# Cross attention with its projections in other places, self-attention with scores 512 columns wide

## The chip, the core and the metric

The kernel runs on one core of a Trainium2 chip. The metric is the device time of one execution in microseconds (us). A core has five engines that the profile names: PE (TensorE, matrix products; its weight loads are listed as PEld), DVE (VectorE), ACT (ScalarE), POOL (GpSimd) and SP, which here only issues DMAs. Each engine works through its own queue in order; an instruction waits at the head of its queue until the semaphores that it names have reached their values, and everything behind it waits with it. PE writes its products to PSUM, which the program hands out in banks of 512 fp32 values for each of 128 partitions; the other engines read them from there.

## The reference, cut to what matters

The program is a decoder of four layers. x is [16, 256, 128] (16 batches of 256 tokens, 128 features), the context ctx is [16, 64, 128]. Each layer has a mixing block, a cross attention against ctx and a feed-forward block, each followed by a residual sum and a layer norm over the 128 features. All that the change touches is softmax attention with 16 heads of 8 features:

```python
q = proj(Q, Wq, bq); k = proj(K, Wk, bk); v = proj(V, Wv, bv)     # heads: [B, 16, S, 8]
scores = einsum('bhqd,bhkd->bhqk', q, k) * (1 / sqrt(8))
attn = softmax(scores, axis=-1)
out = einsum('bhqk,bhkd->bhqd', attn, v)
return merge_heads(out) @ Wo.T + bo
```

Layers 0, 2 and 3 (x0, x2, x3 below) have a cross attention of this kind, with x as Q and ctx as K and V; layer 0's has no bias ahead of Wo, layer 3's adds a mask to the scores. Layer 3 is an encoder block as well: its cross attention is followed by a self-attention in which Q, K and V all come from x (256 keys instead of 64). Layer 1 has other code.

## The kernel before

**Layout.** The residual stream lies in SBUF twice: `xt` with tokens on the partitions, and `xT` with features on the partitions (128 rows, 4096 token columns). A group g is 512 tokens, that is two batches, 2g and 2g+1. `transposed(g)` (L348 to L353) makes a group's part of `xT` from `xt`: four PE transposes (L341) into one PSUM bank `m`, then one ACT copy (L353).

**Heads.** A head has 8 features, so four heads lie in each 32 rows of PE. A product runs in four row tiles i = 0 to 3 of 32 rows; within one tile the four heads j are told apart by a masked copy (`hm4`), which holds the features of one head and zeros for the other three. POOL makes that copy. One of the two operands of the scores must be masked.

**Order.** Each block runs under `in_order`: PE executes its instructions exactly as the program writes them. The other engines' instructions are ordered by a scheduler, by when their data comes. PSUM is handed out by name: in `banks(sc=(2, 2), y=(1, 1), ...)` the first number says how many tiles of that name there are, the second how many banks each has. A new tile takes the place of the oldest of its name and waits until its last reader is done.

**`cross_attention`** (L521) loops over batches b with helpers that are issued ahead of their use:

- `queries(g)` (L554): one product of 512 columns into `m`, and the copy to `qT` on DVE (`evac_dve`, L643 to L648), for two batches.
- `values(g)` (L540): four products into `m` for four batches, spread by DVE into one of two `vx` tiles (L552 with a bias, else L549).
- `keys(b)` (L560): the masked copy `kb` on POOL.
- `scores(b)` (L564): 8 fp32 products `sc<-qT,kb` of 256 columns, then two ACT exponentials of 1024 elements (`e`, L576). With a mask (layer 3), DVE adds it for one half and ACT for the other, ahead of the exponentials.
- `sums(b)` (L585): the products of `e` with `vx` and with ones (`nd`), then `normalized` on DVE: reciprocal (L1967) and product `oTn` (L1969).
- `out_product(b)` (L633): two products `y<-oTn`. After an odd batch `finish` follows: residual sum with a bias (POOL L433, DVE L456 or L1761), `norm` (L384: statistics on DVE L391 and L392, reciprocal root on POOL L379 and L381, `nm` on POOL L396 and L397, four scalings on ACT L402). The scalings are put off to `settle()` in the next round.
- `transposed(b//2-2)` for odd b from 5 on. In layer 0 a `side` runs the end of the layer's mixing block between these steps.

In layers 2 and 3 there are two `nd` tiles and one `m`; in layer 0 one `nd` and two `m`. A round is, on PE: `scores(b+1)`, `sums(b)`, `queries(b//2+1)` in even b, `values(b//4+1)` where b % 4 is 1, `out_product(b-1)`, `transposed` in odd b.

**`self_attention`** (L1854) loops over batches n and head index j, with `aside(n, j)` between the scores of the next step and the sums of this one:

```python
with s.banks(sc=(3, 2), nd=(1, 1), m=(1, 1)), s.in_order():
    ...
            for j in range(4):
                if n < B and (n, j) != (B - 1, 3):
                    scores(n + j // 3, (j + 1) % 4)
                aside(n, j)
                if n < B:
                    sums(n, j)
```

- `scores(n, j)` (L1894) computes one head of each of the four row tiles: for each half t of the keys, the masked keys `kb4` of head j are PE's weights and the 256 queries are streamed. Each of the 8 fp32 products shows as two matmul instructions. Two ACT exponentials follow (L1903).
- `sums(n, j)` (L1905): 8 products with `vxs` (values with columns of ones between), into one `nd` tile for each batch. After j=3: a copy `nds` (DVE L1914), the sums picked out and their reciprocal `rcs` (L1915 to L1918), the numerators `vas` on POOL (L1921, L1922).
- `divided(n)` (L1924): a product `m<-rcs,cst` that swaps columns, then `oTs = vas * m` on DVE (L1928).
- `batch(n)` (L1882): the values of a batch into `m` (`m<-w_x,xT`), four DVE sums into `vxs` (L1888), and the masked keys on POOL (L1892).
- `project` (L1876): `qT` or `kTs` for a group, into `m`, with a DVE copy.
- `out(g)` (L1930): four products into `m`, then `finish` (residual sum L1761, `norm` with the scalings on DVE L405, two products on POOL).

Asides by place, all through the single bank `m`: even n has `project` k at j=0, `divided(n-1)` at j=1, `batch(n+1)` at j=2, `project` q at j=3; odd n has `out` at j=0, `divided` at j=1, `batch` at j=2, `transposed` at j=3.

Of the kernel before, what the change touches and what calls it, by code (L numbers as in the profile page):

```python
# [16 lines left out]
ALU = mybir.AluOpType  # L17
# [503 lines left out]
def cross_attention(s, wq, wk, wv, wo, bq, bk, bv, finish, mask=None, side=None):  # L521

    nc = s.nc
    kT = s.lp.tile([128, B * SC], FP, name=s.nm("kT"))

    vxs = [s.lp.tile([128, 4, 4, 96], FP, name=s.nm("vx")) for _ in range(2)]
    for t in vxs:
        nc.gpsimd.memset(t, 0.0)
    on = s.c["on2"].rearrange("p (u k) -> p u k", u=2)
    hm4 = s.c["hm4"].unsqueeze(2).broadcast_to([128, 4, SC])
    q, kb, es, oT, y = {}, {}, {}, {}, {}

    def values(g):
        ps = s.bank("m")
        for j in range(4):  # L540
            s.mm(ps[:, 128 * j:128 * j + 128], s.ctx2[:, 4 * g + j, :, :].rearrange("p a k -> p (a k)"), wv)
        v = ps.rearrange("p (b i u a d) -> p (b i) u a d", b=4, i=4, u=2, a=2)
        dst = vxs[g % 2].rearrange("p b i (u x) -> p (b i) u x", u=2)
        for a in range(2):
            r = slice(64 * a, 64 * a + 64)
            da = dst[r, :, :, 8 * a:8 * a + 8]
            if bv is None:
                nc.vector.tensor_copy(da, v[r, :, :, a, :])
            else:  # L549
                row = bv[r, :].rearrange("p (i u a d) -> p i u a d", i=4, u=2, a=2)[:, :, :, a, :]  # L550
                for j in range(4):
                    nc.vector.tensor_tensor(da[:, 4 * j:4 * j + 4], v[r, 4 * j:4 * j + 4, :, a, :], row, ALU.add)  # L552

    def queries(g):  # L554
        ps = s.bank("m")
        s.mm(ps, wq, s.xT[:, 512 * g:512 * g + 512])
        q[g] = s.work("qT", [128, 512])
        evac_dve(s, q[g], ps, bq)

    def keys(b):  # L560
        kb[b] = s.work("kb", [128, 4, SC])
        nc.gpsimd.tensor_tensor(kb[b], kT[:, SC * b:SC * b + SC].unsqueeze(1).broadcast_to([128, 4, SC]), hm4, ALU.mult)

    def scores(b):  # L564
        qb = q[b // 2][:, 256 * (b % 2):256 * (b % 2) + 256]
        sc = [s.bank("sc", [128, 2, 2, S]) for _ in range(2)]
        for u in range(2):
            for i in range(4):
                r = slice(32 * i, 32 * i + 32)
                s.mm(sc[i // 2][:, i % 2, u, :],  # L570
                     kb[b][r, 2 * u:2 * u + 2, :].rearrange("p j k -> p (j k)"), qb[r, :])
        e = es[b] = s.work("e", [128, 4, 2, S])
        for h in range(2):
            eu = e[:, 2 * h:2 * h + 2, :, :]
            if mask is None:
                s.latest = nc.scalar.activation(eu, sc[h], AF.Exp, scale=8 ** -0.5)  # L576
            else:
                mk, nmx = mask
                if h == 0:
                    nc.vector.tensor_scalar(eu, sc[h], 8 ** -0.5, mk[:, b:b + 1], ALU.mult, ALU.add)  # L580
                else:
                    nc.scalar.activation(eu, sc[h], AF.Identity, scale=8 ** -0.5, bias=mk[:, b:b + 1])
                s.latest = nc.scalar.activation(eu, eu, AF.Exp, bias=nmx[:, b:b + 1])

    def sums(b):  # L585

        nd = s.bank("nd", [128, 2, S])
        vx = vxs[b // 4 % 2]
        for w in range(2):
            for u in range(2):  # L590
                for i in range(4):
                    s.mm(nd[32 * i:32 * i + 32, w, :], on[:, u, :] if w else vx[:, b % 4, i, 32 * u:32 * u + 32],
                         es[b][:, i, u, :], u == 0, u == 1)
        oT[b] = normalized(s, nd)

    if side is None:
        side = lambda b, late: None
        few, more = 2, 1
    else:
        few, more = 1, 2  # L600
    with s.banks(sc=(2, 2), nd=(few, 1), y=(1, 1), m=(more, 1)), s.in_order(), s.deferring():
        side(-1, False)
        for g in range(2):
            ps = s.bank("nd")
            s.mm(ps, wk, s.ctx2[:, 8 * g:8 * g + 8, 0, :])
            evac(s, kT[:, 512 * g:512 * g + 512], ps, bk)
        values(0)
        side(-1, True)
        queries(0)
        keys(0)  # L610
        keys(1)
        scores(0)
        for b in range(B + 6):
            if b + 1 < B:
                scores(b + 1)
            s.settle()
            side(b, False)
            if b < B:
                sums(b)
            side(b, True)  # L620
            if b + 2 < B:
                keys(b + 2)
                if b % 2 == 0:
                    queries(b // 2 + 1)
                if b % 4 == 1 and b + 3 < B:
                    values(b // 4 + 1)
            if 1 <= b <= B:
                out_product(s, y, oT, b - 1, wo, finish)
            if b % 2 == 1 and b >= 5 and b // 2 - 2 < NG:
                s.transposed(b // 2 - 2)  # L630

# [1222 lines left out]
def self_attention(s, wq, wk, wv, wo, bq, bk, bv, finish):  # L1854
# [5 lines left out]

    nc = s.nc

    vxs = [s.lp.tile([128, 2, 4, 128], FP, name=s.nm("vs")) for i in range(3)]
# [5 lines left out]
    hm4 = s.c["hm4"].unsqueeze(2).broadcast_to([128, 4, S])  # L1871
    lo, hi = s.c["half"][:, 0:1], s.c["half"][:, 1:2]
    row = bv.rearrange("p (i j d) -> p i j d", i=4, j=4)
    q, k, kb, es, oT, nd, va, rc = {}, {}, {}, {}, {}, {}, {}, {}

    def project(d, n, g, wt, bias):  # L1876
        ps = s.bank("m")
# [1 line left out]
        d[g] = s.work(n, [128, 512])  # L1879
        evac_dve(s, d[g], ps, bias)  # L1880

    def batch(n):  # L1882
        ps = s.bank("m", [128, 2, 256])
        for t in range(2):
            s.mm(ps[:, t, 0:128], s.xT[:, S * n + 128 * t:S * n + 128 * t + 128], wv)
        pv = ps[:, :, 0:128].rearrange("p t (i j d) -> p t i j d", i=4, j=4)
        for j in range(4):
            nc.vector.tensor_tensor(vxs[n % 3][:, :, :, 40 * j:40 * j + 8], pv[:, :, :, j, :],  # L1888
                                    row[:, :, j, :].unsqueeze(1).broadcast_to([128, 2, 4, 8]), ALU.add)
        kb[n] = s.work("kb4", [128, 4, S])  # L1890
        o = S * (n % 2)
        nc.gpsimd.tensor_tensor(kb[n], k[n // 2][:, o:o + S].unsqueeze(1).broadcast_to([128, 4, S]), hm4, ALU.mult)  # L1892

    def scores(n, j):  # L1894
        o = S * (n % 2)
        sc = [s.bank("sc", [128, 2, 2, S]) for _ in range(2)]
        for t in range(2):
            for i in range(4):
                r = slice(32 * i, 32 * i + 32)
                s.mm(sc[i // 2][:, i % 2, t, :], kb[n][r, j, 128 * t:128 * t + 128], q[n // 2][r, o:o + S])  # L1900
        e = es[n, j] = s.work("e", [128, 4, 2, S])
        for h in range(2):
            nc.scalar.activation(e[:, 2 * h:2 * h + 2, :, :], sc[h], AF.Exp, scale=8 ** -0.5)  # L1903

    def sums(n, j):  # L1905
        if j == 0:
            nd[n] = s.bank("nd", [128, 2, S])
        for t in range(2):
            for i in range(4):
                s.part(nd[n][32 * i:32 * i + 32, j // 2, :], vxs[n % 3][:, t, i, 32 * j:32 * j + 32],  # L1910
                       es[n, j][:, i, t, :], j == t == 0, j % 2 == 1 and t == 1)
        if j == 3:
            sb = s.work("nds", [128, 2, S])
            nc.vector.tensor_copy(sb, nd[n])  # L1914
            d = rc[n] = s.work("rcs", [128, S])  # L1915
            nc.vector.tensor_scalar(d, sb[:, 0, :], hi, None, ALU.mult)
            nc.vector.scalar_tensor_tensor(d, sb[:, 1, :], lo, d, ALU.mult, ALU.add)
            nc.vector.reciprocal(d, d)  # L1918
            va[n] = s.work("vas", [128, S])
            for u, m in enumerate((lo, hi)):  # L1920
                nc.gpsimd.tensor_scalar(sb[:, u, :], sb[:, u, :], m, None, ALU.mult)  # L1921
            nc.gpsimd.tensor_tensor(va[n], sb[:, 0, :], sb[:, 1, :], ALU.add)  # L1922

    def divided(n):  # L1924
        ps = s.bank("m", [128, 2, S])
        s.mm(ps[:, 0, :], s.c["swap"], rc[n])
        oT[n] = s.work("oTs", [128, S], bufs=4)
        nc.vector.tensor_tensor(oT[n], va[n], ps[:, 0, :], ALU.mult)  # L1928

    def out(g):  # L1930
        y = s.bank("m", [128, 4, D])
# [4 lines left out]
    def aside(n, j):  # L1936

        g = n // 2
        if j == 1 and 1 <= n <= B:
            divided(n - 1)  # L1940
        if j == 2 and n + 1 < B:
            batch(n + 1)
        if n % 2 == 0 and j in (0, 3) and g + 1 < NG:
            project(*((q, "qT", g + 1, wq, bq) if j else (k, "kTs", g + 1, wk, bk)))
        if n % 2 == 1 and j == 0 and 1 <= g <= NG:
            out(g - 1)
        if n % 2 == 1 and j == 3 and 2 <= g <= NG + 1:
# [2 lines left out]
    with s.banks(sc=(3, 2), nd=(1, 1), m=(1, 1)), s.in_order():  # L1950
        project(q, "qT", 0, wq, bq)
        project(k, "kTs", 0, wk, bk)
        batch(0)
        scores(0, 0)
        for n in range(B + 4):
            for j in range(4):
# [49 lines left out]
```

## Time and profile before

| | before |
|---|---|
| time, median of 3 runs | 2239.61 us (2233.31 to 2247.02) |
| the profiled execution: its own time | 2240.24 us |
| the profiled execution: span of the profile | 2238.4 us |
| mean granted PE clock over the span | 0.874 of full speed |
| instructions | 39466 |
| DVE busy groups with most time | L1624 75.1 us, L1967 84.1 us, L391 119.7 us |
| ACT's exponentials in self-attention (L1903) | 128 of 1021 ns |

The profile is of one execution. Its views give times in microseconds from the start of the span. A line of a group or of a timeline names the engine, the program line, the operation, its output and inputs (`out<-in`) with their shapes (partitions x elements), a count (`x16`), and in brackets the idle time of the engine just before with what ended it. "L334" is the helper that issues every plain matrix product, so products are told apart by their tiles. Matmul records of one engine overlap: PE has row tiles that run beside each other, so a step's length is best read from the start of one group to the start of the next. A view by windows gives, for each stretch: the window, its length, busy time and number of instructions of PE, weight loads, DVE, ACT and POOL, then the granted clock, the share of the DMA engines and their rate.

### The profile page before, as it was taken

What the parts mean: (1) busy time and instruction counts of PE and PEld (TensorE: products, weight loads), DVE (VectorE), ACT (ScalarE), POOL (GpSimd) and SP (SyncE); (2) the same over time, 40 slices, a digit from 0 to 9 for tenths busy, and PEclk for the clock granted to TensorE, in tenths of its full rate; (3) what the DMA queues carried; (4) which work ended last, traced back from release to release, by engine and by line L of the source; (5) the groups of instructions that cost most, each with busy time, mean ns of one, the idle gap of its engine ahead of it and who ended that gap; (6) DMA issues with size and microseconds to landing.
All of it is one profiled execution on the core that took longest, in us unless ns stands there. A gap on an engine that the chain in (4) does not pass through costs nothing.

```text
span 2238.4 us, 39466 instructions
## 1 busy us (share of the span) xinstructions
PE 1801.0 (80%) x16572; PEld 1135.4 (51%) x16572; DVE 1133.3 (51%) x2808; ACT 857.8 (38%) x1267; POOL 810.5 (36%) x956
## 2 busy tenths in 40 slices
PE   6784378886999826859784799987879998999998
PEld 3451256664777714636452566654445544555554
DVE  5677625554466663145476767746725552322231
ACT  6565633432433201322353222225646654233221
POOL 2432322222344225756334334434535653121110
PEclk8896579997999956979896789988979998999999
DMA  3000000001001212430000000010000000000000
GB/s 113 4 3 21 1 2 3 3 2 45 11 29 29 66 46 47 78 82 1 6 15 20 1 1 1 2 36 29 2 1 2 2 1 1 5 5 5 5 10 10
DMA packets 45649, 41.59 MB, mean 19 GB/s; under 512 B 6880, under 2 KB 42144, under 8 KB 44832
## 3 DMA queue, kind: packets, MB, share of 16 engines
q1 hardware_dynamic: 35456, 31.22, 4.5%
q0 software_dynamic: 5632, 4.33, 1.5%
q10 hardware_dynamic: 4384, 3.52, 0.5%
q8 instruction: 130, 2.13, 0.4%
q14 instruction: 47, 0.39, 0.1%
HBM read 28.44 MB, written 10.62 MB: 17 GB/s over the span
## 4 chain that ended last, share of the span: by engine, by line
PE 55%; DVE 16%; POOL 12%; issue 9%; ACT 5%; DMA 2%; POOLq 0%; SPq 0%; DVEq 0%; ACTq 0%
PE p L334 14%; PE m L334 12%; PE sc L334 11%; PE y L334 6%; PE nd L334 3%; POOL rs L381 2%; PE nd L338 2%; DVE rcT L1967 2%; PE den L338 2%; PE m L341 2%; POOL acc L1316 2%; DVE st L391 1%; PE num L334 1%; ACT xt L402 1%; DVE r L456 1%
## 5 line engine op out<-in xcount | busy, mean ns | idle before, releaser
L334 PE MATMUL p<-h,w_f 128*128 128x512 f32 x512 | 222.3, 592 | 0.4 <-DVE h L1818 0.4
L334 PE MATMUL sc<-qT,kb 32*128 32x256 f32 (+1 forms) x2816 | 182.8, 378 | 42.5 <-DVE qT L648 16.1
L379 POOL TENSOR_SCALAR ve<-mv 128x4 f32<-128x4 f32 x128 | 30.5, 238 | 425.9 <-DVE mv L392 422.4
L334 PEld LDWEIGHTS sc<-qT,kb 32*128 32x128 f32 x2816 | 127.7, 201 | 94.4 <-issue 61.1
L341 PE MATMUL m<-ident,xt 128*128 128x128 f32 x448 | 87.8, 319 | 104.7 <-ACT xt L402 48.4
L334 PEld LDWEIGHTS p<-h,w_f 128*128 128x128 f32 x512 | 96.7, 190 | 119.8 <-issue 117.9
L1903 ACT ACTIVATE e<-sc 128x1024 f32<-128x1024 f32 x128 | 124.0, 1021 | 74.2 <-PE sc L334 73.4
L381 POOL TENSOR_TENSOR rs<-ve,nhalf 128x4 f32<-128x4 f32 x128 | 134.0, 1047 | 6.3
L341 PEld LDWEIGHTS m<-ident,xt 128*128 128x128 f32 x448 | 59.3, 156 | 133.5 <-ACT xt L402 55.6
L391 DVE BATCH_NORM_STATS2 st<-r 128x6 f32<-128x128 f32 x480 | 119.7, 272 | 3.2
L433 POOL TENSOR_TENSOR xb<-xt,r_x 128x512 f32<-128x512 f32 x48 | 60.8, 1272 | 155.9 <-DVE r L1761 78.4
L1967 DVE RECIPROCAL rcT<-nd 128x256 f32<-128x256 f32 x48 | 84.1, 1751 | 64.5 <-PE nd L334 64.5
L353 ACT COPY xT<-m 128x512 f32<-128x512 f32 x104 | 59.9, 581 | 134.0 <-PE m L341 133.4
L402 ACT ACTIVATE xt<-r,nm,rs 128x128 f32<-128x128 f32 x176 | 72.5, 484 | 94.7 <-POOL nm L397 63.7
L1823 ACT ACTIVATE h<-p,w_f 128x512 f32<-128x512 f32 x64 | 44.0, 687 | 163.4 <-PE p L334 163.3
L334 PE MATMUL m<-xT,w_a 128*128 128x512 f32 x144 | 81.7, 682 | 25.8 <-DVE vxs L908 18.8
L405 DVE TENSOR_SCALAR xt<-r,mv,rs 128x128 f32<-128x128 f32 x208 | 65.8, 378 | 59.6 <-POOL rs L381 59.6
L1829 DVE TENSOR_TENSOR ys<-y,r_f 128x512 f32<-128x512 f32 x8 | 5.5, 691 | 175.4 <-PE y L334 175.4
L576 ACT ACTIVATE e<-sc 128x1024 f32<-128x1024 f32 x64 | 61.9, 1019 | 62.8 <-PE sc L334 62.8
L1624 DVE TENSOR_TENSOR a<-sc,cst 128x1024 f32<-128x1024 f32 x64 | 75.1, 1209 | 14.7 <-PE sc L334 14.7
L392 DVE BATCH_NORM_AGGREGATE mv<-st 128x2 f32<-128x6 f32 x512 | 80.9, 167 | 0.1
L1092 ACT ACTIVATE e<-sc 128x1024 f32<-128x1024 f32 x32 | 32.8, 1024 | 110.0 <-PE sc L334 110.0
(423 smaller groups left out, 4086.3 us busy)
## 6 DMA issues: line engine op xcount, KB each, us to landing
acc<-xt SPq DMA_DIRECT2D x16, 256.0 KB, 2.8
mw<-in_moe SPq DMA_DIRECT2D x8, 512.0 KB, 3.7
yx<-acc SPq DMA_DIRECT2D x12, 256.0 KB, 3.4
w_f<-in_w_f SPq DMA_DIRECT2D x1, 2824.0 KB, 10.6
w_x<-in_w_x SPq DMA_DIRECT2D x1, 2336.5 KB, 9.8
xt<-in_x SPq DMA_DIRECT2D x8, 256.0 KB, 7.4
rows<-xn SPq DMA_DIRECT2D x8, 256.0 KB, 2.4
out_x<-xt SPq DMA_DIRECT2D x8, 256.0 KB, 2.3
```

Source lines behind the costliest of these rows:

```text
L334: self.put(self.nc.tensor.matmul(out=out, lhsT=lhsT, rhs=rhs, start=start, stop=stop))
L338: self.put(self.nc.tensor.matmul(out=out, lhsT=lhsT, rhs=rhs, start=start, stop=stop, skip_group_check=True))
L341: self.put(self.nc.tensor.transpose(out, in_, self.ident if ident is None else ident))
L381: nc.gpsimd.tensor_tensor(rs, ve, self.nhalf[:, :n], ALU.pow)
L391: nc.vector.bn_stats(st[:, j, :], r[:, j, :])
L392: nc.vector.bn_aggr(mv[:, j, :], st[:, j, :])
L402: ins, front = nc.scalar.activation(out[:, j, :], r[:, j, :], AF.Identity, bias=nm[:, j:j + 1], scale=rs[:, j:j + 1]), self.latest
L405: ins, front = nc.vector.tensor_scalar(out[:, j, :], r[:, j, :], mv[:, j, 0:1], rs[:, j:j + 1], ALU.subtract, ALU.mult), self.mark
L576: s.latest = nc.scalar.activation(eu, sc[h], AF.Exp, scale=8 ** -0.5)
L1624: s.mark = nc.vector.tensor_tensor(a[:, h, :, :], sc[h].rearrange("p i j k -> p (i j) k"), tri, ALU.mult)
L1903: nc.scalar.activation(e[:, 2 * h:2 * h + 2, :, :], sc[h], AF.Exp, scale=8 ** -0.5)
L1967: s.nc.vector.reciprocal(rc, nd[:, 1, :])
```

## The change

In `cross_attention` two calls move within a round: `queries(b//2+1)` from after the sums to before them, in the same even rounds; `values(b//4+1)` from the rounds with b % 4 = 1 to those with b % 4 = 2, and from before `out_product` to after it.

In `self_attention` the mask goes to the other operand: POOL makes masked queries `qb` (tile name still `kb4`) instead of masked keys. The weights of a scores product are then 128 keys without a mask, and the streamed operand is two heads' masked queries, 512 columns. A step (n, j) now holds the key half t = j % 2 for two heads instead of both halves for one head; there are 4 products of 512 columns for 8 of 256. `sums` follows this order with the same products. `divided(n-1)` and `batch(n+1)` now share one `m` tile, a half of the bank each, one behind the other at j=1. `project` q is at j=0 of even n and k at j=2; j=3 of even n and j=2 of odd n have no aside.

```diff
@@ cross_attention, the loop over b
             s.settle()
             side(b, False)
+            if b % 2 == 0 and b + 2 < B:
+                queries(b // 2 + 1)
             if b < B:
                 sums(b)
             side(b, True)
             if b + 2 < B:
                 keys(b + 2)
-                if b % 2 == 0:
-                    queries(b // 2 + 1)
-                if b % 4 == 1 and b + 3 < B:
-                    values(b // 4 + 1)
             if 1 <= b <= B:
                 out_product(s, y, oT, b - 1, wo, finish)
+            if b % 4 == 2 and b + 2 < B:
+                values(b // 4 + 1)
             if b % 2 == 1 and b >= 5 and b // 2 - 2 < NG:
                 s.transposed(b // 2 - 2)
@@ self_attention
-    def batch(n):
-        ps = s.bank("m", [128, 2, 256])
+    def batch(n, ps):
         for t in range(2):
-            s.mm(ps[:, t, 0:128], s.xT[:, S * n + 128 * t:S * n + 128 * t + 128], wv)
+            s.mm(ps[:, t, :], s.xT[:, S * n + 128 * t:S * n + 128 * t + 128], wv)
...
-        kb[n] = s.work("kb4", [128, 4, S])
+        qb[n] = s.work("kb4", [128, 4, S])
         o = S * (n % 2)
-        nc.gpsimd.tensor_tensor(kb[n], k[n // 2][:, o:o + S].unsqueeze(1).broadcast_to([128, 4, S]), hm4, ALU.mult)
+        nc.gpsimd.tensor_tensor(qb[n], q[n // 2][:, o:o + S].unsqueeze(1).broadcast_to([128, 4, S]), hm4, ALU.mult)
 
     def scores(n, j):
-        o = S * (n % 2)
+        o = S * (n % 2) + 128 * (j % 2)
         sc = [s.bank("sc", [128, 2, 2, S]) for _ in range(2)]
-        for t in range(2):
-            for i in range(4):
-                r = slice(32 * i, 32 * i + 32)
-                s.mm(sc[i // 2][:, i % 2, t, :], kb[n][r, j, 128 * t:128 * t + 128], q[n // 2][r, o:o + S])
+        for i in range(4):
+            r = slice(32 * i, 32 * i + 32)
+            s.mm(sc[i // 2][:, i % 2, :, :].rearrange("p h k -> p (h k)"), k[n // 2][r, o:o + 128],
+                 qb[n][r, j - j % 2:j - j % 2 + 2, :].rearrange("p h k -> p (h k)"))
...
-        for t in range(2):
+        t = j % 2
+        for u in range(2):
             for i in range(4):
-                s.part(nd[n][32 * i:32 * i + 32, j // 2, :], vxs[n % 3][:, t, i, 32 * j:32 * j + 32],
-                       es[n, j][:, i, t, :], j == t == 0, j % 2 == 1 and t == 1)
+                h = j - t + u
+                s.part(nd[n][32 * i:32 * i + 32, j // 2, :], vxs[n % 3][:, t, i, 32 * h:32 * h + 32],
+                       es[n, j][:, i, u, :], j == u == 0, t == u == 1)
...
-    def divided(n):
-        ps = s.bank("m", [128, 2, S])
-        s.mm(ps[:, 0, :], s.c["swap"], rc[n])
+    def divided(n, ps):
+        s.mm(ps, s.c["swap"], rc[n])
         oT[n] = s.work("oTs", [128, S], bufs=4)
-        nc.vector.tensor_tensor(oT[n], va[n], ps[:, 0, :], ALU.mult)
+        nc.vector.tensor_tensor(oT[n], va[n], ps, ALU.mult)
...
     def aside(n, j):
 
         g = n // 2
-        if j == 1 and 1 <= n <= B:
-            divided(n - 1)
-        if j == 2 and n + 1 < B:
-            batch(n + 1)
-        if n % 2 == 0 and j in (0, 3) and g + 1 < NG:
-            project(*((q, "qT", g + 1, wq, bq) if j else (k, "kTs", g + 1, wk, bk)))
+        if j == 1 and n <= B:
+            ps = s.bank("m", [128, 2, S])
+            if n >= 1:
+                divided(n - 1, ps[:, 0, :])
+            if n + 1 < B:
+                batch(n + 1, ps[:, 1, :].rearrange("p (t c) -> p t c", t=2))
+        if n % 2 == 0 and j in (0, 2) and g + 1 < NG:
+            project(*((q, "qT", g + 1, wq, bq) if j == 0 else (k, "kTs", g + 1, wk, bk)))
```

More of the change, by code (lines that the diff above doesn't have):

```diff
@@ L1873, in self_attention @@
     row = bv.rearrange("p (i j d) -> p i j d", i=4, j=4)
-    q, k, kb, es, oT, nd, va, rc = {}, {}, {}, {}, {}, {}, {}, {}
+    q, k, qb, es, oT, nd, va, rc = {}, {}, {}, {}, {}, {}, {}, {}
     def project(d, n, g, wt, bias):
@@ L1880, in project @@
         evac_dve(s, d[g], ps, bias)
-    def batch(n):
-        ps = s.bank("m", [128, 2, 256])
+    def batch(n, ps):
         for t in range(2):
-            s.mm(ps[:, t, 0:128], s.xT[:, S * n + 128 * t:S * n + 128 * t + 128], wv)
-        pv = ps[:, :, 0:128].rearrange("p t (i j d) -> p t i j d", i=4, j=4)
+            s.mm(ps[:, t, :], s.xT[:, S * n + 128 * t:S * n + 128 * t + 128], wv)
+        pv = ps.rearrange("p t (i j d) -> p t i j d", i=4, j=4)
         for j in range(4):
@@ L1952, in self_attention @@
         project(k, "kTs", 0, wk, bk)
-        batch(0)
+        batch(0, s.bank("m", [128, 2, S])[:, 1, :].rearrange("p (t c) -> p t c", t=2))
         scores(0, 0)
```

## The prediction

> **What bounds the kernel.** The page first: busy shares, one figure per engine for the whole program.
>
> ```profile
> PE 1801.0 (80%) x16572; PEld 1135.4 (51%) x16572; DVE 1133.3 (51%) x2808; ACT 857.8 (38%) x1267; POOL 810.5 (36%) x956
> ```
>
> TensorE leads, but the change touches four stages only, so I asked for busy time in those windows (columns: window, length, PE, weight loads, DVE, ACT, POOL, granted clock): layer 0's, 2's and 3's cross attention, then self-attention.
>
> ```profile
> 65.00:177.00 112.00, 85.38 (x952) 53.13 (x952) 71.75 (x181) 62.45 (x106) 39.00 (x72) 0.91 0.03 8
> 1086.00:1181.00 95.00, 77.56 (x902) 45.85 (x901) 60.73 (x150) 45.10 (x64) 29.55 (x49) 0.95 0.03 9
> 1516.00:1629.00 113.00, 85.00 (x901) 48.22 (x900) 79.08 (x162) 67.28 (x84) 53.62 (x84) 0.88 0.01 1
> 1635.00:1839.00 204.00, 193.03 (x2260) 105.55 (x2261) 98.08 (x250) 126.91 (x134) 107.80 (x96) 0.96 0.01 2
> ```
>
> Self-attention is PE from end to end (193 of 204 us): whatever PE waits there is added to the time. In the cross attentions no engine is full; a loop over engines sets the pace. Next the timeline of one odd batch n of self-attention (start, us, instruction, idle time before and its releaser).
>
> ```profile
> 1733.84 1.15 PE L334 MATMUL sc<-qT,kb 32*128 32x256 f32 x16
> 1734.92 0.70 PE L334 MATMUL m<-rcs,cst 128*128 128x256 f32 x2
> 1735.55 1.07 PE L338 MATMUL nd<-e,vs 128*32 128x256 f32 x16
> 1736.55 1.15 PE L334 MATMUL sc<-qT,kb 32*128 32x256 f32 x16
> 1739.00 0.71 PE L334 MATMUL m<-w_x,xT 128*128 128x128 f32 x4 [1.31 <-DVE oTs L1928]
> ...
> 1737.50 1.11 DVE L405 TENSOR_SCALAR r<-r,mv,rs 128x128 f32<-128x128 f32 x4 [1.50 <-POOL rs L381]
> 1738.54 0.41 DVE L1928 TENSOR_TENSOR oTs<-vas,m 128x256 f32<-128x256 f32 x1
> ```
>
> Scores last 1.08 us start to start, sums 1.00, `divided` (m<-rcs) 0.63, `batch` (m<-w_x,xT) 0.64. `batch` takes the single bank m that oTs still reads, and oTs stands on DVE behind the whole finish of `out`. PE lost 1.31 us.
>
> **Self-attention, part by part.**
>
> *Wide scores.* 64 score steps go from 16 matmuls of 256 columns (two for each fp32 product) to 8 of 512. Sixteen instructions with a mean of 410 ns fit into 1.08 us because row tiles run beside each other. The nearest row to the new form is the projection m<-xT,w_x, 128x512, two instructions: 1720.07 to 1721.12, 1.05 us. So half as many instructions, each streaming twice as long, with the loads hidden both times. The Trainium skill ("TensorE: Matmul & The Clock Gate", Back-to-back issue gap) gives about 81 ns a matmul at 128 columns and 131 at 512 in a stream; put 256 at about 98 on that line, and two 256 become one 512 at a third less: 0.36 us x 64 = 23 us gained, an estimate from that page. The bounds are -23 and +1; I take the row: 1.08 against 1.05 plus the tiles' stagger, -0.4 us in all. Sums keep their count and shapes; the masked copy on POOL (1.89 us) keeps its size and place in POOL's order.
>
> *Two asides in one bank.* `divided` and `batch` now follow each other at j=1 in the two halves of one bank. The built program shows what this means: `batch`'s first matmul waits for the count that oTs raises. The page "PSUM — Partial Sum Buffer" (summary of rules) speaks against sharing: a matmul should go to another bank than the one being read, guarded by bank and not by address. Without that guard the halves would be independent, the 1.31 us waits (six, at n = 3 to 13) would go and the merged run would save about 0.19 us of switching sixteen times: -11 us. With it, the wait stays where DVE puts it, and the two steps that covered part of it now come after. I take the guarded sum:
>
> Odd n with an `out` before it. Let R be the end of sums(n-1,3), 1730.68 here. oTs ends at 1738.95, R+8.27, by DVE's and POOL's chain alone (copy, reciprocal 1.75, `out`'s residual and statistics, POOL's pow, four scalings, oTs 0.41). `batch` starts at R+8.32, now as before. Before, sums and scores (1.00+1.08) were done ahead of it; now they come after it. So +2.08. The next even n: `divided` to the end of oTs is 1747.52 to 1748.74; `batch` can start 1.27 us after `divided`, where it took 0.63: +0.64. Queued behind the waiting matmul: all of PE, and behind it ACT's exponentials.
>
> *Empty slots.* j=3 of even n and j=2 of odd n have no aside now. Scores that follow sums directly meet ACT, which needs 2x1.02 us a step: at 1694.4, such a place, scores took 1.30 for 1.08: +0.22. In even n it disappears in the later wait, in odd n it shows.
>
> A pair is +2.08+0.64+0.22 = +2.9 us, six pairs 17.6; n=0 to 2 add about 2; minus 0.4: **+19**.
>
> *The clock.* PE idles in each odd n from about R+4.8 to R+8.32, some 3.5 us. What idling does is seen in layer 2:
>
> ```profile
> 1149.82 0.63 PE L341 MATMUL m<-ident,xt 128*128 128x128 f32 x4 [1.95 <-DVE vx L552]
> ...
> 1147.46:1150.87 3.41, 1.46 (x16) 1.12 (x18) 3.06 (x12) 1.99 (x5) 0.48 (x1) 1.00 0.00 0
> 1150.87:1154.28 3.41, 3.41 (x37) 1.56 (x36) 0.00 (x0) 2.14 (x3) 0.61 (x1) 0.50 0.02 5
> ```
>
> After 1.95 us idle in one 3.41 us window, the next is granted half speed; the same 1.6 us of work was lost twice in layer 3. The 1.31 us waits never did it. A 3.5 us wait leaves 1.75 us or more in some window wherever it falls; 1.2 to 1.7 us are lost each time, six times: **+8** (bounds 0 and +10). Self-attention: +27.
>
> **Cross attention.** Timeline of a pair of batches in layer 2 (b=6):
>
> ```profile
> 1132.11 0.61 PE L334 MATMUL y<-w_x,oTn 128*128 128x128 f32 x4
> 1133.76 1.15 PE L334 MATMUL sc<-qT,kb 32*128 32x256 f32 x16 [1.04 <-DVE qT L648]
> ...
> 1137.25 0.60 PE L341 MATMUL m<-ident,xt 128*128 128x128 f32 x4
> 1137.78 1.15 PE L334 MATMUL sc<-qT,kb 32*128 32x256 f32 x16
> ...
> 1137.84 1.65 ACT L402 ACTIVATE xt<-r,nm,rs 128x128 f32<-128x128 f32 x4 [0.92 <-POOL nm L397]
> 1139.40 0.56 ACT L353 COPY xT<-m 128x512 f32<-128x512 f32 x1
> ```
>
> The change moves `queries` ahead of sums: its copy no longer sits behind the reciprocal, and the wait for qT (7.8 us in layer 2, 8.3 in layer 3, 8.4 in layer 0) goes. What is late next: from b=5 on a `transposed` fills m's only bank in layers 2 and 3, and ACT empties it behind the four norm scalings. Let T be the end of sums(b), b even, here 1131.15. Copy xT ended at T+8.81; without the query copy (0.55 net) on DVE it ends at T+8.26. PE gets there early: y 0.61, scores 1.08, sums 1.87, y 0.55, transpose 0.53, scores 1.08 = T+5.7. Then queries waits 2.6 us, and with it sums(b+2), for which nothing is missing. The next T is 8.3+0.96+1.87 = T+11.1; it was 9.57. The built program bears the wait out: four queries in each of these layers (b=6 to 12) wait for that copy.
>
> Against it, `values` leaves odd b. There the transpose waited 1.95 us for it at b=5 and 9 (pairs of 12.8, and 14.2 with the slow clock); at even b it has more time: with it a pair is 11.3.
>
> Layer 2: 0 to 4 -1.5, 4 to 6 -1.7, 6 to 8 +1.7, 8 to 10 -3.1, 10 to 12 +1.7, end -1; two new idle gaps of 2.6 us at half clock about +1.8: **-2**. Layer 3 has 1.28 us of mask on DVE ahead of the last statistics and three activations a batch on ACT (9.0 us a pair): the copy ends at T+9.5, with values T+10.4, so pairs of 12.4 and 13.3 where 14.3, 10.1, 14.1, 10.1 were measured from b=4: +2.8 in four, -3 in the others, 0; idle gaps of 2.3 to 3.1 us, with the clock lost on three of four, +4: **+4**. Layer 0 has two banks m, so queries waits for an earlier copy, about 1 us; three early pairs (11.6, 11.6, 13.1) shrink to DVE's 10.3 to 11 (-4.5), the later ones about even: **-4**. Sum -2, bounds -15 and +12. If the early copies did not hide values' DVE work (8 adds, 1.4 us), it would show once per move, nine times.
>
> **Sum.** The profiled execution took 2240.24 us around its span of 2238.4: +27-2 = +25, 2265 us. The median of the three runs, 2239.61, differs by less than a microsecond.
>
> **Rivals.**
> - *Forecast* (0.50): the bank holds PE, the cross attentions even out: 2265.
> - *Query waits stay hidden, not slower* (0.10): m is free before queries asks. Its place is ACT's copy at T+8.3; it decides from T+5.7 downward. Then all 24.5 us of qT waits go, with 7.8 of values waits and 4.8 of slow clock: -37+27, 2230. For it: those waits end last on PE today. Against: norm scalings start at T+6.7 today and only 0.55 comes off.
> - *Wide scores pay* (0.08), by the page's stream figures: 2242. Against it the 512 row.
> - *Clock holds* (0.15): no half-speed windows in self-attention: about 2257. For it: one 1.95 us wait in layer 2, at 1125.7, fell across two windows and cost nothing.
> - *Cross attention loses* (0.17): each later query wait drops the clock and layer 0 gains nothing: +12 for -2, 2279.
> That the asides don't share the bank is excluded by the built program.
>
> **Numbers.** About 1% (22 us, so 2217 and 2262) is what a measurement of this kernel can tell from no change. Slower: 0.38 of the forecast, the last rival, 0.05 of the clock's: 0.60. Faster: 0.04, from the second. Same: 0.36. The range runs from the wide scores' 2242 to a little past 2279, for the spread of runs.
>
> **What would show it.** Scores' row: 8 matmuls of 32x512, still near 1.08 us a step. m<-w_x,xT in odd n: idle 3.4 us or so before it, releaser oTs; in even n 0.6. Granted clock of the self window falling from 0.96 to about 0.9. Queries from b=6 in layers 2 and 3: released by ACT's xT copy, with the qT waits gone. Wrong if scores take clearly under 1 us, if `batch` follows `divided` without a gap, or if the self window grows by under 12 us.

## The result, and the profile after

The changed kernel takes **2276.11 us** (median of 4 runs, 2271.25 to 2279.85), the one before 2242.07 in the same comparison: 1.0138 times as long, 95% interval 1.0109 to 1.0168. The forecast was 2265.0, with a range of 2242 to 2283. The profiled execution took 2274.99 us, 34.8 more than that of before (2240.24).

The page's busy shares of the changed kernel:

```profile
PE 1824.1 (80%) x16060; PEld 1119.2 (49%) x16060; DVE 1132.8 (50%) x2808; ACT 857.4 (38%) x1267; POOL 810.8 (36%) x956
```

There are 512 fewer matmuls, and yet PE is busy 23 us longer. At half clock the same products count as busy for longer (1.91 us instead of 1.07 for the sums in the last timeline of this section), so busy time alone does not say whether work was added. The same four windows as before, moved to where the stages now stand (columns: window, length, PE, weight loads, DVE, ACT, POOL, granted clock, DMA share, GB/s):

```profile
64.00:176.00 112.00, 87.51 (x952) 52.61 (x949) 72.23 (x183) 62.14 (x106) 37.85 (x72) 0.91 0.03 8
1094.00:1189.00 95.00, 80.22 (x902) 45.36 (x901) 60.36 (x150) 44.67 (x64) 29.65 (x49) 0.93 0.03 9
1523.00:1640.00 117.00, 89.74 (x905) 50.61 (x904) 79.88 (x162) 67.35 (x84) 54.35 (x85) 0.85 0.01 1
1646.50:1873.00 226.50, 200.46 (x1748) 83.25 (x1749) 98.09 (x250) 126.91 (x134) 108.07 (x96) 0.93 0.00 1
```

Self-attention is some 22 us longer, with the clock down from 0.96 to 0.93; layer 0 and layer 2 have not moved, layer 3's cross attention is about 4 us longer. For the rest of this document a stage's length is the time between the starts of the same two DVE instructions in each trace, so that stages can be compared between kernels. These stretches reach beyond the windows above (layer 2's begins some 40 us earlier and ends 20 later) and take in neighbouring code that is the same in all kernels (us; the last column is the time of that profiled execution):

| kernel | layer 0 cross | layer 1 self | layer 2 cross | layer 3 cross | layer 3 self | execution |
|---|---|---|---|---|---|---|
| before | 124.0 | 131.7 | 156.3 | 150.3 | 205.6 | 2240.24 |
| after | 124.0 | 139.7 | 155.8 | 153.9 | 228.0 | 2274.99 |

The touched stages sum to +25.5. Another 8.0 us are in layer 1, whose code is the same in both. How far a stage moves with its code unchanged can be read from the other profiles: layer 0 is at 124.0 in all with its old code, layer 2 at 154.3 to 156.3, layer 3 at 150.3 to 150.5, self-attention at 204.2 to 205.7. The -0.5 of layer 2 lies within that. The timeline of an odd batch of self-attention, after (start, us, instruction, idle time before and its releaser), PE first, then DVE:

```profile
1720.33 1.37 PE L334 MATMUL sc<-kb,kTs 32*128 32x512 f32 x8
1721.62 1.16 PE L334 MATMUL m<-w_x,oTs 128*128 128x128 f32 x8
1722.71 1.07 PE L338 MATMUL nd<-e,vs 128*32 128x256 f32 x16
1723.71 1.14 PE L334 MATMUL sc<-kb,kTs 32*128 32x512 f32 x8
1724.78 0.70 PE L334 MATMUL m<-rcs,cst 128*128 128x256 f32 x2
1728.64 1.12 PE L334 MATMUL m<-w_x,xT 128*128 128x128 f32 x4 [3.16 <-DVE oTs L1930]
...
1727.15 1.11 DVE L405 TENSOR_SCALAR r<-r,mv,rs 128x128 f32<-128x128 f32 x4 [1.50 <-POOL rs L381]
1728.18 0.41 DVE L1930 TENSOR_TENSOR oTs<-vas,m 128x256 f32<-128x256 f32 x1
```

`divided` ends at 1725.48, and `batch`, in the other half of the same bank, waits 3.16 us for `oTs`. On DVE `oTs` stands behind the four scalings L405, which wait for POOL. A wide scores step lasts 1.07 us (1723.71 to 1724.78); after a step without an aside it lasts 1.29 (the row at 1720.33). In even batches `oTs` runs at once, and the wait is short:

```profile
1742.30 0.71 PE L334 MATMUL m<-w_x,xT 128*128 128x128 f32 x4 [0.58 <-DVE oTs L1930]
```

What the long wait does to the clock, in two windows of 3.41 us of the changed kernel:

```profile
1725.39:1728.80 3.41, 0.25 (x2) 0.16 (x2) 1.70 (x8) 1.50 (x2) 2.10 (x4) 1.00 0.00 0
1728.80:1732.22 3.42, 3.42 (x24) 1.79 (x28) 0.61 (x4) 0.00 (x0) 2.09 (x2) 0.50 0.00 0
```

PE was busy for 0.25 us in the first window, and was granted half speed in the next, where it had work for all of it. But not every wait of this length costs the clock. There are six, and two of them, which are split between two windows, are followed by full speed. Below, a wait of 3.28 us and then one of 3.17; each leaves 1.59 us of work in its first window, and half speed follows only the first:

```profile
1694.67:1698.08 3.41, 1.59 (x10) 0.43 (x10) 1.76 (x10) 1.94 (x2) 3.17 (x4) 1.00 0.01 2
1698.08:1701.50 3.42, 1.96 (x12) 1.32 (x16) 2.03 (x9) 0.00 (x0) 2.18 (x2) 0.50 0.00 0
...
1752.70:1756.11 3.41, 1.59 (x10) 0.43 (x10) 1.87 (x10) 1.94 (x2) 3.15 (x4) 1.00 0.00 0
1756.11:1759.52 3.41, 2.05 (x24) 1.25 (x28) 1.92 (x9) 0.00 (x0) 2.28 (x2) 1.00 0.02 5
1759.52:1762.94 3.42, 3.42 (x36) 1.37 (x28) 0.00 (x0) 2.46 (x3) 2.17 (x2) 1.00 0.00 0
```

Last, b=6 of layer 2's cross attention, PE and ACT:

```profile
1129.10 0.60 PE L341 MATMUL m<-ident,xt 128*128 128x128 f32 x4
1129.63 1.15 PE L334 MATMUL sc<-qT,kb 32*128 32x256 f32 x16
1133.73 1.13 PE L334 MATMUL m<-xT,w_x 128*128 128x512 f32 x2 [2.95 <-ACT xT L353]
1134.78 1.91 PE L334 MATMUL nd<-e,vx 128*32 128x256 f32 x16
...
1131.56 1.65 ACT L402 ACTIVATE xt<-r,nm,rs 128x128 f32<-128x128 f32 x4 [2.77 <-POOL nm L397]
1133.11 0.56 ACT L353 COPY xT<-m 128x512 f32<-128x512 f32 x1
```

The qT wait is gone. `queries` now waits for the bank that the transpose filled, until ACT has copied it behind its scalings; and the sums that follow run at half speed (1.91 for 1.07).

### The profile page after: what moved, and what is told of

It reads as the page before. It is cut to its first block, busy times and chain, and to the rows that moved or that the text cites. A ratio compares the mean times of both kernels' runs of the same rounds, so it can differ in the third digit from the quotient of the medians.

```text
span 2273.0 us, 38447 instructions
## 1 busy us (share of the span) xinstructions
PE 1824.1 (80%) x16060; PEld 1119.2 (49%) x16060; DVE 1132.8 (50%) x2808; ACT 857.4 (38%) x1267; POOL 810.8 (36%) x956
## 4 chain that ended last, share of the span: by engine, by line
PE 56%; DVE 15%; POOL 12%; issue 9%; ACT 5%; DMA 2%; POOLq 0%; DVEq 0%; SPq 0%; ACTq 0%
PE p L334 14%; PE m L334 13%; PE sc L334 11%; PE y L334 6%; PE nd L334 3%; POOL rs L381 3%; PE nd L338 3%; PE den L338 2%; DVE st L391 2%; PE m L341 2%; PE num L334 1%; DVE r L456 1%; POOL acc L1316 1%; ACT xt L402 1%; PE o L338 1%
## 5 line engine op out<-in xcount | busy, mean ns | idle before, releaser
L1904 ACT ACTIVATE e<-sc 128x1024 f32<-128x1024 f32 x128 | 124.0, 1021 | 96.7 <-PE sc L334 94.8
L334 PE MATMUL sc<-qT,kb 32*128 32x64 f32 (+1 forms) x1792 | 108.6, 364 | 19.3 <-POOL kb L892 7.9
L334 PEld LDWEIGHTS sc<-qT,kb 32*128 32x128 f32 x1792 | 80.8, 213 | 42.4 <-POOL kb L892 12.2
L405 DVE TENSOR_SCALAR xt<-r,mv,rs 128x128 f32<-128x128 f32 x208 | 65.7, 377 | 59.8 <-POOL rs L381 59.8
L576 ACT ACTIVATE e<-sc 128x1024 f32<-128x1024 f32 x64 | 61.9, 1019 | 56.9 <-PE sc L334 56.9
L334 PE MATMUL sc<-kb,kTs 32*128 32x512 f32 x512 | 80.9, 670 | 0.0
```

What stands on the lines that cost most here:

```text
L334: self.put(self.nc.tensor.matmul(out=out, lhsT=lhsT, rhs=rhs, start=start, stop=stop))
L405: ins, front = nc.vector.tensor_scalar(out[:, j, :], r[:, j, :], mv[:, j, 0:1], rs[:, j:j + 1], ALU.subtract, ALU.mult), self.mark
```

## The experiments

**One half of the change each.** The first kernel has the changed `cross_attention` and the old `self_attention`, the second the reverse.

> Only the cross attention's half of the change: queries ahead of the sums, values in even rounds; self-attention as before. The forecast's theory (each half stands for itself; the cross attentions lose in the later queries waits what they gain early): layers 0, 2, 3 at 0, 0 and +4 us against before, the whole within 5 us of before, about 2245. The rival that the forecast named (the cross attention loses): +12, about 2254. The profile after also shows 8 us more in layer 1's self-attention, which no line of the change touches: if the shifted cross attention of layer 0 sets the phase there, this kernel shows those 8 us too (about 2253, all of it in layer 1); if they fall by chance, they come and go between kernels that share layer 0's code.

> Only the self-attention's half: wide scores and the two asides in one bank; the cross attentions as before. The forecast's theory: +22 us in self-attention (as the profile after has it, against 27 forecast), so about 2264, with PE waits of 3.2 us on oTs in each odd batch and four to six half-speed windows of the clock. Rival (the two halves act on each other, or the extra time of layer 1 belongs to the change): clearly under +15 or over +30. Layer 0's code is that of before here: a layer 1 that is 8 us long again would speak for chance.

Measured: the cross attentions alone 1.0034 (1.0010 to 1.0058) of before, 2250.72 against 2241.18; the self-attention alone 1.0113 (1.0082 to 1.0145), 2268.93. The halves add up to the whole within their intervals. In the profiles the first has layers 0, 2 and 3 at 123.6, 155.0 and 155.0 (-0.4, -1.3, +4.7: +3.0), and layer 1 at 144.3 (+12.6), without which the whole would lie within the 5 us that were expected; the second has self-attention at 228.2, as the whole change has.

**One half of the self-attention's change each.** One kernel has the wide scores with the asides of before, the other the shared bank with the old scores.

```diff
-        if j == 1 and n <= B:
-            ps = s.bank("m", [128, 2, S])
...
+        if j == 1 and 1 <= n <= B:
+            divided(n - 1)
+        if j == 2 and n + 1 < B:
+            batch(n + 1)
```

> Self-attention with wide scores alone: 512 columns, masked queries, sums in the new order; divided and batch keep their own tiles and their places at j=1 and j=2, project q and k and the empty slots as before; cross attention as before. The forecast's theory: -0.4 us, the same 1.31 us waits on oTs, no half-speed window: 2242, nothing to measure. Rival (wide scores pay, half the matmuls at a third less): -15 to -23, about 2222. Rival (wide scores cost, by the later first use of a head's second key half or by ACT): +5 or more.

> Self-attention with the asides alone: divided and batch in two halves of one bank at j=1, project q at j=0 and k at j=2; scores of 256 columns with masked keys as before; cross attention as before. The forecast's theory: all of the self-attention's loss is here, +22 to +27, about 2266, with the 3.2 us waits on oTs. Rival (the wide scores carry part of the loss): under +12.

Measured: the shared bank alone has the whole loss, self-attention 228.2 us, 1.0105 (1.0086 to 1.0123). That this is the same 228.2 as with the wide scores added is in part chance: the stage begins at half speed for 15.6 us here and for 8.7 there, and later there are 10.2 us of half speed here and 20.5 there. The wide scores alone have 207.2 us, 1.0021 (1.0006 to 1.0036): no gain, but +1.6 us where -0.4 was expected. The timeline of an odd batch of the kernel with wide scores alone shows what lengthens its pairs of batches (25.05 us for 24.31; PE, DVE, POOL):

```profile
1737.55 0.70 PE L334 MATMUL m<-rcs,cst 128*128 128x256 f32 x2 [0.58 <-DVE r L1761]
...
1733.53 1.11 DVE L1920 TENSOR_SCALAR rcs<-nds,cst 128x256 f32<-128x256 f32 x1
...
1732.60 1.89 POOL L1894 TENSOR_TENSOR kb<-qT,cst 128x1024 f32<-128x1024 f32 x1 [7.36 <-DVE qT L648]
```

POOL's masked copy is now made of queries, and queries are projected at j=3 in the old order of asides: the copy starts only at 1732.60, when the sums have just ended, and DVE's first step of the reciprocal stretches from 0.35 us (every other such row) to 1.11 until POOL is done at 1734.49. `out`'s residual comes 0.75 us later, and `divided` waits 0.58 us for its bank in six batches. The six pairs are 4.4 us longer in all; the start of the stage is 2.9 us shorter (see the part on self-attention's ends). The change as a whole avoids the longer pairs, since it projects q at j=0.

**The idle stretch filled.** This is the changed kernel with more work in it:

```diff
     def divided(n, ps):
-        s.mm(ps, s.c["swap"], rc[n])
+        for _ in range(5 if n % 2 == 0 and 2 <= n < B - 2 else 1):
+            s.mm(ps, s.c["swap"], rc[n])
```

> The changed kernel with work added: the product divided (m<-rcs,cst) is issued five times instead of once in the odd batches n = 3 to 13, with the same operands into the same half bank, so that PE computes through most of the 3.2 us in which it waits for oTs. 24 products of 0.63 us more, 15 us of PE work. Theory (the idle stretch is what halves the clock): batch starts when it did, since oTs comes by DVE's chain; the half-speed windows of self-attention go, and the stage falls from 228 us to 221 to 224: more work, less time, about 2271. Rival (the clock has other reasons): half-speed windows stay, 228 to 230 us. Rival (PE waits longer behind the repeated products): 232 or more.

Measured: self-attention **220.0 us against 228.0, with 24 products more**; 1.0093 (1.0067 to 1.0118) of before, where the change had 1.0138. Its timeline in an odd batch:

```profile
1722.00 2.43 PE L334 MATMUL m<-rcs,cst 128*128 128x256 f32 x10
1725.86 0.71 PE L334 MATMUL m<-w_x,xT 128*128 128x128 f32 x4 [1.43 <-DVE oTs L1931]
```

The whole of its self-attention in one window (length, PE, weight loads, DVE, ACT, POOL, clock):

```profile
1646.00:1866.00 220.00, 203.80 (x1798) 89.53 (x1799) 99.11 (x250) 127.20 (x135) 109.20 (x98) 0.98 0.00 1
```

`batch` starts 8.31 us after the sums of the batch before (1717.55), exactly where it did in the changed kernel. PE idles 1.43 us instead of 3.16, the clock stays at 0.98, and no window behind the stage's first 7.0 us is at half speed; the changed kernel has 20.5 us of it there, and 8.5 at the start. So the idle stretch is what halved it, and that was worth nearly all of the 8.0 us.

**oTs ahead of the scalings.** Here the changed kernel stands with two DVE items in another order. `out`'s scalings are put off (the mechanism that the cross attention has) until `oTs` is issued, and held behind it:

```diff
-        nc.vector.tensor_tensor(oT[n], va[n], ps, ALU.mult)
+        s.mark = nc.vector.tensor_tensor(oT[n], va[n], ps, ALU.mult)
...
                 divided(n - 1, ps[:, 0, :])
+            s.settle()
+            s.due = s.mark = None
...
+            s.due = []
             out(g - 1)
```

> The changed kernel, with one order of DVE changed: in odd batches oTs runs ahead of out's four norm scalings instead of behind them (which wait for POOL's reciprocal root and stand in its way). Nothing else moves on PE. Theory (the loss is DVE's place for oTs, which the shared bank hands on to PE): the wait of batch in odd n falls from 3.2 us to 0.7 to 1.0, as in even n 0.6, the clock stays up, self-attention 228 us to 208 to 212, about 2258. Rival (the shared bank costs for itself, by turning twice at one place): over 220 us.

Measured: self-attention **204.6 us**, 23.4 below the changed kernel and no longer than before (205.6; 204.2 to 205.7 over the profiles with the old code). An odd batch on PE and DVE:

```profile
1724.63 0.70 PE L334 MATMUL m<-rcs,cst 128*128 128x256 f32 x2
1725.92 0.71 PE L334 MATMUL m<-w_x,xT 128*128 128x128 f32 x4 [0.58 <-DVE oTs L1930]
...
1725.44 0.42 DVE L1930 TENSOR_TENSOR oTs<-vas,m 128x256 f32<-128x256 f32 x1
1726.99 1.11 DVE L405 TENSOR_SCALAR r<-r,mv,rs 128x128 f32<-128x128 f32 x4 [1.13 <-POOL rs L381]
```

The bank is shared as in the changed kernel, and costs 0.58 us a batch. `oTs` fits into the time in which DVE waits for POOL anyway, and the scalings end no later. So most of the loss was not the bank by itself but the queue position of the instruction that frees it. Not all of it: the last kernel below has the same order on DVE with the asides of before, where `divided` and `batch` take the bank in turn, a step apart. A pair of batches takes 23.07 us there against 24.66 here. Two waits of 0.58 and two scores steps of +0.22 after an empty slot make up these 1.6 us. The whole kernel is at 1.0035 (1.0016 to 1.0054), 2255.98 against 2246.04; what is left over before lies in layer 3's cross attention (154.0) and in layer 1 (143.9).

**One move of the cross attention each.** One kernel moves only `values`, one only `queries`; the self-attention is the old one.

> Of the change, only the move of values in the cross attentions (to even rounds, after out_product); queries and self-attention as before. Theory: the transposed product of b = 5 and 9 no longer waits 1.95 us for values' DVE work, but values now waits about 1 us for queries' copy in the same bank: pairs of 12.8 and 14.2 us in layer 2 become 10.5. Layer 2 -6, layer 3 -4, layer 0 -1; about 2231. Rival (the wait only moves): 0.

> Of the change, only the move of queries in the cross attentions (ahead of the sums); values and self-attention as before. Theory: up to b = 4 it gains the 1.2 us of each qT wait, from b = 6 on queries waits 1.2 to 3 us for ACT's copy of the transpose in the single bank, and the values waits stay: layer 2 +4, layer 3 +7, layer 0 0; about 2252. Rival (the query waits were the limit): -5 or less.

Measured: `values` alone **gains**, 0.9941 (0.9920 to 0.9961), 2232.08 against 2246.04; `queries` alone loses, 1.0070 (1.0035 to 1.0106), 2259.21. Layer by layer, against before:

| kernel | layer 0 | layer 2 | layer 3 |
|---|---|---|---|
| values moved | +2.9 | -6.2 | -6.4 |
| queries moved | +6.1 | +6.1 | +6.5 |
| both moved | -0.4 | -1.3 | +4.7 |

The waits of PE in layer 2 (us in total, times, longest), with values moved:

```profile
PE sc L334 <- DVE qT L648: 4.3, 4, 1.1
PE m L334 <- DVE qT L648: 2.8, 3, 0.9
```

and with queries moved:

```profile
PE m L334 <- ACT xT L353: 5.6, 2, 2.8
PE m L341 <- DVE vx L552: 4.2, 2, 2.3
```

With values moved, three of the seven qT waits became waits of `values` for the bank (2.8 us), and the 3.9 us of the transposes for `vx` are gone. With queries moved these stay, and 5.6 us of waits for ACT's copy come on top, for 7.5 of the 7.8 us of qT waits that went. All its waits in layer 2 together grew by only 0.8 us; but the stage is at half speed for 45.9 us instead of 36.3, and half of that difference, 4.8 us (an estimate), with the waits nearly makes the +6.1. The sizes were off in places: layer 3 gained more from values than expected (-6.4 for -4), layer 2 lost more from queries (+6.1 for +4), and layer 0 lost 2.9 and 6.1 where about nothing was expected; that the two together lose nothing there was not foreseen and was not followed further.

**Layer 1.** One kernel has the change in layer 0's cross attention only; the other is the kernel before.

> The change's two moves in layer 0's cross attention alone; layers 2 and 3 and the self-attention as before. It is to tell whether the longer layer 1 (self-attention a1, 139.7 to 144.3 us in the four kernels with the changed layer 0, 131.7 to 137.9 in the four with the old one; its own code is the same in all) comes with layer 0's change. If it does: layer 0 at 0, layer 1 at 139 to 145, the whole +5 to +7, about 2250. If it falls by chance: layer 1 anywhere from 131 to 145 and the median within 3 us of before.

> The kernel before once more, for a second profile of layer 1. If the length of layer 1 belongs to the code ahead of it: 131 to 138 us. If it falls by chance: as likely 139 to 145.

Measured: with layer 0's moves alone 1.0037 (1.0013 to 1.0061), 2251.47 against 2242.58. Layer 0 itself is at 124.0, unmoved; layer 1 at 140.0. The kernel before has 131.7 again. Layer 1 in one window (length, PE, weight loads, DVE, ACT, POOL, clock), of before:

```profile
274.00:405.00 131.00, 103.54 (x2223) 73.96 (x2225) 52.06 (x102) 51.96 (x72) 39.23 (x39) 0.86 0.01 2
```

of after:

```profile
274.00:405.00 131.00, 105.24 (x2067) 74.25 (x2070) 48.51 (x98) 49.05 (x69) 33.78 (x34) 0.79 0.01 2
```

of the kernel with layer 0's moves:

```profile
274.00:405.00 131.00, 104.10 (x2088) 73.74 (x2089) 50.63 (x100) 49.29 (x69) 36.33 (x37) 0.81 0.01 2
```

and of before's second profile:

```profile
274.00:405.00 131.00, 103.53 (x2232) 73.96 (x2234) 51.92 (x102) 51.95 (x72) 39.14 (x39) 0.86 0.01 2
```

The same code gets a clock of 0.86 or of 0.79 to 0.81 and gets 135 to 156 fewer matmuls done in the same 131 us. Over thirteen profiles: with the changed layer 0 139.7, 144.3, 143.8, 143.9, 140.0; with the old one 131.7 twice, 137.6, 137.9, 137.3, and 140.6 in the combined kernel below; with one of the moves 140.0 and 133.3. So layer 0's change tends to come with a longer layer 1, by more half-speed windows, and the +8.9 us of that kernel (medians; interval 2.9 to 13.7) have no other touched or lengthened place of that size in its profile. But the combined kernel has the old layer 0 and a long layer 1, and of the twelve executions with layer 0's moves two took only 2234 us, less than any of the fifteen of before (2237 to 2248).

The traces point to where the clock's windows of 3.41 us fall. Layer 1 begins at half speed, and that stretch ends 33.1 us after the stage's start in the combined kernel, with layer 0's moves and with values moved: three different layers 0, and layer 1 takes 140.6, 140.0 and 140.0. In before's two profiles it ends after 34.0 us, and layer 1 takes 131.7 in both. This does not sort all thirteen (the wide scores alone: 33.9, and 137.9), and no run moved the windows by themselves. What decides it, and whether layer 0's change does, stays open.

**Put together.** The last kernel moves `values` in layers 2 and 3, and `queries` there only up to b = 4; layer 0 as before; self-attention as before with `oTs` ahead of the scalings.

```diff
+            if free and b % 2 == 0 and b <= 4:
+                queries(b // 2 + 1)
             if b < B:
                 sums(b)
...
+            if free and b % 4 == 2 and b + 2 < B:
+                values(b // 4 + 1)
```

> What the runs so far point to, put together. Layers 2 and 3: values in even rounds after out_product, queries ahead of the sums only for b = 0, 2, 4 (while no transpose fills the bank m yet), behind them from b = 6 on. Layer 0: cross attention as before. Self-attention: scores and asides as before, but oTs on DVE ahead of out's norm scalings in odd batches. Theory: layer 2 -7.5 (values -6.2, early queries -1.3), layer 3 -8, self-attention -7 (six waits of 1.31 us go), layer 1 as with layer 0's old code: 2246 - 22, about 2224 on this chip. Rival (values alone and early queries exclude each other, as queries and values do in the change): layers 2 and 3 at -3 each, about 2233.

Measured: **2219.70 against 2242.58, 0.9864 (0.9803 to 0.9924)**, faster than the kernel before, and so than the change. Layer 2 148.5 (-7.8), layer 3 140.1 (-10.2), self-attention 198.5 (-7.1; of its waits for `oTs`, 7.9 us before, one of 0.6 is left), against a layer 1 of 140.6 in this profile.

## Why the prediction held, and where it did not

*The shared bank: right, place and size.* The prediction had `batch` at R+8.32 after the end of the sums; measured R+8.31 (1720.33 to 1728.64). The even step was given as +0.64, and the wait that makes it is 0.58; the scores after an empty slot as +0.22, measured 1.29 for 1.07. A pair of batches was to grow by 2.9 us from 24.31; in the filled kernel, where the clock doesn't mix in, it is 27.24, +2.93. The rule that the prediction took from the Trainium skill ("PSUM — Partial Sum Buffer", Summary: rules for kernel authors), to guard by bank, is what the program does: in both wait rows above `batch` waits for the reader of the bank's other half.

*Wide scores: right.* -0.4 us for 64 steps by the nearest row, 1.07 against 1.08 measured, and no gain where they stand alone. The estimate of 23 us from the page's stream figures was the wrong one to take here.

*The clock: right in mechanism, in size by some luck.* +8 was given, 8.0 measured by filling the gap. But it was to come from all six waits, at 1.2 to 1.7 us each. PE's idle stretch was 3.16 us where about 3.5 was said, so that it can be split between two windows, and two of the six cost nothing; the other four cost 1.5 to 2.5 us each against the filled kernel, two of them with two windows at half speed. With the shared bank alone only two of the six cost the clock anything.

*Self-attention's ends: mis-sized.* The stage was to lose 27 and lost 22.4. The six pairs' sum is right; the term "n=0 to 2 add about 2" left out the start of the stage. From the first projection's copy to the first `out` it took 46.3 us before and 43.8 after. Masked queries do not wait for the projection of k, so the first scores start without the 0.75 us for POOL's copy and the 0.27 for ACT that they waited before. And the half speed with which the stage begins ends 8.5 us after that copy instead of 15.6, which is worth some 3.5 us (an estimate, half of the difference). It goes with the masked queries: 7.0 to 8.7 us in all five kernels that have them, 12.5 to 15.7 in the others. The +2 of the prediction less these 4.5 us is the -2.5 measured.

*Cross attention, layers 2 and 3: right in mechanism, near in sum.* The four queries waits of layer 2 are 2.95, 1.23, 2.78 and 1.23 us, where the prediction worked out 2.6; the shorter ones come after a round with `values` in it. Layer 2 was given -2 and has -0.5 (-1.3 with the cross attentions alone), layer 3 +4 and has +3.6 (+4.7). Half-speed windows after the longer gaps appear as said, at 1134.78 above. Pair by pair it was further off: the pairs b=4 to 6 and 8 to 10 of layer 2 were to shrink by 1.7 and 3.1 us, with about 0.9 each lost again to the clock; from reciprocal to reciprocal they went from 12.57 to 13.15 and from 14.24 to 13.14.

*Cross attention, layer 0: wrong.* -4 was given, 0.0 measured. The waits came as said; the step that failed is that the three early pairs would shrink to 10.3 to 11 us. The waits of PE in layer 0, before:

```profile
PE sc L334 <- DVE qT L646: 8.4, 8, 1.5
PE m L334 <- ACT xT L353: 1.8, 1, 1.8
```

and after:

```profile
PE m L334 <- ACT xT L353: 7.4, 6, 2.1
PE nd L334 <- DVE oTn L1973: 8.4, 9, 2.2
```

The first of the six waits for `xT` is there before as well (1.8 us). The five new ones last 0.6 to 1.6 us, about 1 each as forecast; the qT waits of 8.4 went, and in their place came these and longer waits for the single `nd` (6.4 us to 8.4). From reciprocal to reciprocal the three pairs took 9.39, 11.65 and 12.41 us, for 11.58, 11.56 and 13.13: 2.8 us less. But the first reciprocal came 2.6 us later in the stage. The second product of `queries` now stands ahead of the first sums, where the clock is still at half speed, and takes 2.0 us there, a cost that the prediction had at nothing:

```profile
75.39 2.08 PE L334 MATMUL m<-xT,w_x 128*128 128x512 f32 x2
```

The four later pairs were about even, as said (44.8 us before, 44.9 after).

*Not in the sum at all:* layer 1. Its 8.0 us make up most of the difference between the touched stages' +25.5, where +25 was forecast, and the +34.8 of the two executions. That the forecast for what the change touches was right to a microsecond is luck in part: two misses cancelled (self-attention 4.6 less than given, layer 0 4 more). The measured total is further off, by a stage that no line of the diff names.

Of the rivals, "wide scores pay" and "clock holds" fall with the wide scores alone and with the filled gap, "query waits stay hidden" with the waits shown. "Cross attention loses" (+12) is not what the touched layers show (+3.0).

## What to carry to other kernels

Putting two results into one bank makes the second product wait for the reader of the first. What that costs is set by where this reader stands in its engine's queue, so look there first: one DVE item moved ahead of work that waited anyway gave back 23 us. Moved in the kernel before, where a step lies between the two products, it gained 7 us, and against that the two in one place still lost 1.6 us a pair. Work ahead of its use pays only until the next resource in the chain is late; here that was a bank which ACT empties, and moving the other of two projections alone would have gained. And a gap on PE can cost twice, once as a wait and once at half speed afterwards.

## What the runs showed of the hardware

Adding 24 products to a waiting PE made a stage 8.0 us shorter, since PE kept its clock. A gap that leaves PE only 0.25 us of work in a window of 3.41 us is followed by half speed; a gap of 1.43 us in the filled kernel was not. In between it depends on how the gap falls on the windows: with 1.59 us of work in one, half speed followed at 1698.08 and full speed at 1756.11. The Trainium skill ("TensorE: Matmul & The Clock Gate", Why this matters for your kernels) says to leave no gap over about 3 us; the wait of 1.95 us in layer 2 of before, shown in the prediction, already cost one.

DVE and POOL got in each other's way: a DVE step of 0.35 us took 1.11 while POOL made its copy of 1.89 us. The skill ("Trainium Architecture — The Big Picture", What this means for kernel authors) says that the two share a port by an exclusive lock; the row fits that, and shows what it costs when such a copy is moved behind a late input.
